# First attention of a four-layer sequence: scores computed a second time with keys on partitions, maxima added by a matmul, exponentials no longer turned

## Chip, cores and metric

The kernel runs on one core of a Trainium2 chip. The metric is the device time of one execution in microseconds; lower is better. The program has four layers; the change touches the first alone, a cross-attention over 16 batches.

## The reference

Layer 0 is a cross-attention with grouped keys. For each of 16 batches, 100 rows of queries (32 heads of 16 channels) look at 361 context rows (8 key and value heads, each shared by four query heads):

```python
q = hidden_state @ Wq + bq                     # (16, 100, 512), 32 heads of 16
k = encoder_hidden_state @ Wk + bk             # (16, 361, 128), 8 heads of 16
v = encoder_hidden_state @ Wv + bv
scores = jnp.einsum('bkgld,bksd->bkgls', q, k) * scale      # scale = 1/4
scores = scores + encoder_attention_mask[:, :, None, :, :]  # a mask per batch, row and key
attn = jax.nn.softmax(scores, axis=-1)
out = jnp.einsum('bkgls,bksd->bkgld', attn, v)
x = out.reshape(b, l, H) @ Wo + bo + hidden_state
return (x - mu) * jax.lax.rsqrt(var + EPS) * gamma + beta
```

Layers 1 and 3 are recurrent blocks, layer 2 is another cross-attention with a feed-forward part. They are not changed. All data is float32.

## The kernel before

Everything is pinned: the helpers `mm` (line 94), `turn` (a transpose on TensorE, line 97) and the wrapped engines `vector`, `scalar`, `gpsimd` (line 89) keep instructions in the order in which the program writes them, engine by engine. So nearly all instructions of the first layer have line 89, 94 or 97 in the profile, and one tells them apart by their tiles.

A batch has 32 heads. A key projection `kz` is written twice, once with the odd and once with the even key heads set to zero (`par01`, a column of ones and zeros per parity), so that a block of 32 partitions holds one key head that counts. Eight steps `x` per batch (two parities `par` by four query groups `q`) make four score tiles each, one for each block `r` of 32 partitions:

- `scores`: four matmuls of 32 rows in four different row groups of the array, which run side by side (a burst), into a ring of four PSUM banks `l0_sc`; rows on partitions, 361 keys along the free axis. Each matmul in float32 is two passes in the profile, so a burst is eight.
- `maximum(r)`: one VectorE instruction adds the mask, writes the negated scores to `pr`, and puts the row's negated maximum into a column of `nm`. In the profile it is CUSTOM_DVE_ANT_0, with a DVE_READ_ACCUMULATOR2_ANT that brings out the maximum.
- `exp(r)`: ScalarE takes the exponential with that maximum as its bias, in place, with the row sum in a column of `sums`.
- `turn_weights`: for the step before, TensorE turns the 100 x 361 weights in three pieces of 121 keys (4 turns a piece, 12 a step) into a ring of two banks `l0_pT`, and ScalarE (two pieces) and VectorE (one) copy them to `pt`, where keys are on partitions.
- `attend`: weights times values, 32 columns of the array per block, summed over both parities in the bank `acc`. The values `vz` have zeros in the other parity's columns.
- `invert` and `divide`: reciprocal of the 32 sums per row, spread to channels by GpSimd, turned by four transposes, multiplied into `y`.
- `output`: four matmuls with `wo`, then the residual, the norm's statistics, scale and shift.

Projections, attend, divide and output are cut into pieces, each with an estimated time and a slot from which it may run; `Filler.run` deals them out to the 24 slots of a batch (three a step) in equal shares, one TensorE piece after another, between the bursts. One bank `m` serves all projections in turn.

Eight PSUM banks: four for scores, two for turned weights, one `acc`, one `m`. The next burst needs all four score banks, and of these the last is freed by the fourth maximum, which stands on VectorE behind the copy of turned weights (cut to the order of calls):

```python
maximum(0)
maximum(1)
due = fill.run(3 * x, due + share)
if last:
    turn_weights(*last[:3], 0)(scalar.copy)
exp(0); exp(1); maximum(2)
due = fill.run(3 * x + 1, due + share)
if last:
    turn_weights(*last[:3], 1)(vector.tensor_copy)
maximum(3)
```

Layer 2's attention (around lines 1550 to 1712) is built in another way: it takes maxima of a first set of scores into a shared scratch tile, turns them, and computes the scores again with keys on partitions.

Of the kernel before, what the change touches and what calls it, by code (L numbers as in the profile page):

```python
# [37 lines left out]
def xattn_sequence(ctx: ExitStack, tc: tile.TileContext, d: dict, out: bass.AP):  # L38
# [313 lines left out]
    def layer0(next_weights, next_small):  # L352
        with ExitStack() as es:
            one = es.enter_context(tc.tile_pool(name="l0_one", bufs=1))
            two = es.enter_context(tc.tile_pool(name="l0_two", bufs=2))
            score = psum_ring(es, "l0_sc", 4)
            turned = psum_ring(es, "l0_pT", 2)
# [10 lines left out]
            par01 = one.tile([128, 2], F32, name="l0_par")  # L368
            bqs = one.tile([128, 4], F32, name="l0_bqs")
            kb = one.tile([128, 2], F32, name="l0_kb")  # L370
            vzs = [one.tile([KW, 3, 2, 128], F32, name=f"vz{i}") for i in range(2)]

            live, qzs, xTs = {}, {}, {}

            def load(b):
                ct = two.tile([128, NC, S2], F32, tag="ct", name=f"ct_{b}")
                nc.sync.dma_start(
                    out=ct,
                    in_=d["ctxT"][:, b * S2 : (b + 1) * S2].rearrange("(c p) s -> p c s", p=128),
                )  # L380
                mask = two.tile([L, S2], F32, tag="mask", bufs=3, name=f"mask_{b}")
                nc.sync.dma_start(out=mask, in_=d["mask0"][b])
                nc.sync.dma_start(out=xb[b], in_=d["x"][b])
                live[b] = {"ct": ct, "mask": mask}
# [81 lines left out]


            def scores(b, x):
                par, q = x // 4, x % 4
                t = live[b]  # L470
                if x == 0:
                    t["nm"] = two.tile([L, 32], F32, tag="nm", name=f"nm0_{b}")
                    t["sums"] = two.tile([L, 32], F32, tag="sums", name=f"sums_{b}")
                    gpsimd.memset(t["sums"], 0.0)
                sl = slice(b % G * L, (b % G + 1) * L)
                ss = [score() for r in range(4)]
                for r in BURST:
                    rs = slice(32 * r, 32 * r + 32)
                    mm(
                        out=ss[r][:L, :S2], lhsT=qzs[b // G][rs, q, sl], rhs=t["kz"][rs, par, :],  # L480
                        start=True, stop=True,
                    )
                pr = two.tile([L, 4, S2], F32, tag="pr", bufs=3, name=f"pr_{b}_{x}")

                def maximum(r):

                    col = 8 * q + 2 * r + par
                    vector.tensor_tensor_reduce(
                        out=pr[:, r, :], in0=ss[r][:L, :S2], in1=t["mask"], scale=-1.0, scalar=FLT_MAX,
                        op0=ALU.add, op1=ALU.min, accum_out=t["nm"][:, col : col + 1],  # L490
                    )

                def exp(r):
                    col = 8 * q + 2 * r + par
                    scalar.activation(
                        pr[:, r, :], pr[:, r, :], AF.Exp, bias=t["nm"][:, col : col + 1], scale=-1.0,
                        accum_out=t["sums"][:, col : col + 1],
                    )

                return pr, maximum, exp  # L500

            def turn_weights(b, x, pr, j):

                par, q = x // 4, x % 4
                t = live[b]
                if q == 0 and j == 0:
                    t["pt", par] = two.tile([KW, 3, 4, T], F32, tag="pt", name=f"pt0_{b}_{par}")
                ps = turned()
                k0 = KEYS[j][0]
                for r in range(4):  # L510
                    turn(ps[:KW, r * L : (r + 1) * L], pr[:, r, k0 : k0 + KW], ident[:L, :L])
                return lambda copy: copy(
                    t["pt", par][:, j, :, q * L : (q + 1) * L],
                    ps[:KW, :T].rearrange("p (r t) -> p r t", t=L),
                )

            def attend(fill, b, par, j, slot):
                n = KEYS[j][1]
                first, last = par == 0 and j == 0, par == 1 and j == 2

                def step():
                    t = live[b]
                    if first:
                        t["acc"] = ps_acc.tile([128, 512], F32, tag="acc", name=f"acc_{b}")
                    for r in range(4):
# [3 lines left out]
                            rhs=t["pt", par][:n, j, r, :], start=first, stop=last,  # L529
                        )  # L530

                def then():
                    t = live[b]
                    t["y"] = two.tile([128, T], F32, tag="y", bufs=1, name=f"y0_{b}")
                    scalar.copy(t["y"], t["acc"][:, :T])

                fill.add(0.8, slot, step, then if last else None, 0)

            def invert(b):

                t = live[b]
                rinv = two.tile([L, 32], F32, tag="rinv", name=f"rinv_{b}")
                vector.reciprocal(rinv, t["sums"])
                t["rx"] = two.tile([L, E], F32, tag="rx", bufs=1, name=f"rx_{b}")
                gpsimd.tensor_copy(
                    t["rx"].rearrange("p (h c) -> p h c", c=16), rinv[:, :, None].to_broadcast([L, 32, 16])
                )

            def divide(fill, b, slot):
                rb = []  # L550

                def step():
                    rb.append(bank(f"rb_{b}"))
                    for q in range(4):
                        turn(
                            rb[0][:, q * L : (q + 1) * L], live[b]["rx"][:, q * 128 : (q + 1) * 128],
                            ident[:L, :L],
                        )

                def then():  # L560
                    y = live[b]["y"]
                    vector.tensor_tensor(y, rb[0][:, :T], y, ALU.mult)

                fill.add(0.5, slot, step, then, 1, object())

            def output(fill, b, slot):
# [6 lines left out]
                def then(t):  # L573
# [3 lines left out]
                    fill.later.append((fill.slot + 2, stats))  # L577

                def stats():
                    st["mv"], st["rstd"] = ln_stats(two, [st["v"]], 1e-6, f"0_{b}", vector, gpsimd)  # L580
                    fill.later.append((fill.slot + 4, scaled))

                def scaled():
# [9 lines left out]
                    fill, 0.88, slot, ps, lambda q: live[b]["y"][:, q * L : (q + 1) * L],  # L593
# [16 lines left out]
            vector.tensor_scalar(kb, par01, bk, None, ALU.mult)  # L610
            for t in vzs:
                gpsimd.memset(t, 0.0)
# [14 lines left out]


            last = None
            for b in range(B + 1):  # L630
                more, more2, prev = b + 1 < B, b + 2 < B, b > 0
                g, bi = b // G, b % G
                if b < B:
                    if more2:
                        load(b + 2)
                    if bi == 0 and g + 1 < NG:
                        load_x(g + 1)
                    if prev:
                        gpsimd.tensor_tensor(xb[b], xb[b], rows[:, 0, :], ALU.add)
                if more:  # L640
                    keys(fill, b + 1)
                if b == 0:
                    values(fill, 0)
                if prev:
                    for j in range(3):
                        attend(fill, b - 1, 1, j, 3 + j)
                if more:
                    values(fill, b + 1, 6)
                if prev:
                    divide(fill, b - 1, 7)  # L650
                    output(fill, b - 1, 9)
                if b < B:
                    for j in range(3):
                        attend(fill, b, 0, j, 15 + j)
                    if bi < 3 and g + 1 < NG:
                        for q in ((0, 1), (2,), (3,))[bi]:
                            queries(fill, g + 1, q, 6)
                share = fill.total() / 24
                due = 0.0
                for x in range(8):  # L660
                    now = (b, x, *scores(b, x)) if b < B else None
                    if now:
                        pr, maximum, exp = now[2:]
                        maximum(0)
                        maximum(1)
                    due = fill.run(3 * x, due + share)
                    if last:
                        turn_weights(*last[:3], 0)(scalar.copy)
                    if now:
                        exp(0)  # L670
                        exp(1)
                        maximum(2)
                    due = fill.run(3 * x + 1, due + share)
                    if last:
                        turn_weights(*last[:3], 1)(vector.tensor_copy)
                    if now:
                        maximum(3)
                    if last:
                        turn_weights(*last[:3], 2)(scalar.copy)
                    if now:  # L680
                        exp(2)
                        exp(3)
                    last = now
                    due = fill.run(3 * x + 2, due + share)
# [1262 lines left out]
```

## Time and profile before

| | |
|---|---|
| three runs | 3127.76, 3128.34 (median), 3133.83 us |
| the profiled execution | 3127.86 us, of which the span of instructions is 3126.1 us |
| granted TensorE clock, mean | 0.961 |
| first scores of the first layer | 39.35 us |
| first instruction of layer 1 that follows the last row of layer 0 | 677.41 us |
| busy in the span: TensorE, VectorE, ScalarE, GpSimd | 91%, 54%, 42%, 37% |
| busy between 39.3 and 677.4 us | 577.0, 361.0, 451.7, 85.4 us |

The page shows one profiled execution. A group line has the line, the engine (PE is TensorE's matmul, PEld its weight load, DVE VectorE, ACT ScalarE, POOL GpSimd), the operation, the tile written and the tiles read, shapes, and the count; behind the bar the busy time of the group, the mean of one in ns, the idle time ahead of it and what ended most of that. Timeline lines start with the start and the length in us. Matmul ends are modelled, so the start of the next group says better how long PE was held.

### The profile page before, as it was taken

The page shows a single profiled execution, that of the slowest core. Times are in us where ns is not written, and L with a number is a line of the kernel's source. Part 1 is how long each engine was busy: PE and PEld are TensorE (multiplying, and loading weights), DVE is VectorE, ACT ScalarE, POOL GpSimd, SP SyncE. Part 2 cuts the span into 40 slices and gives each one's busy share as a digit, 9 for nine tenths or more (in the row PEclk, how much of TensorE's full clock was granted, in tenths as well). Part 3 has the DMA queues.
Part 4 walks back from the last instruction along what each step waited for, and adds up shares of the span by engine and source line. Part 5 has one row for each costly group of instructions (what it writes and reads, how often), then busy time and mean ns, then how long its engine had stood idle before and what let it go on. Part 6 is the DMA issues. An engine that isn't in the chain of part 4 may idle for free. (4 is left out here: it accounts for less than half of the span.)

```text
span 3126.1 us, 44079 instructions
## 1 busy us (share of the span) xinstructions
PE 2858.8 (91%) x16323; PEld 1488.0 (48%) x16323; DVE 1675.5 (54%) x3507; ACT 1308.6 (42%) x2921; POOL 1159.3 (37%) x953
## 2 busy tenths in 40 slices
PE   6999999878889999989999999989999789999998
PEld 3555555534344444444555555455555344444444
DVE  2555556553989988433333333331000369998981
ACT  3777677753435355422222232221111335344553
POOL 0111111133777777412222111220000367787771
PEclk9999999989999999989999999999999889999999
DMA  6010101013224353230000001020002323324321
GB/s 196 24 34 24 34 24 37 3 39 116 80 77 129 96 161 87 71 88 21 21 22 21 21 21 34 28 71 11 11 11 62 101 63 106 109 76 155 105 60 56
DMA packets 139561, 195.93 MB, mean 63 GB/s; under 512 B 23974, under 2 KB 106854, under 8 KB 139346
## 3 DMA queue, kind: packets, MB, share of 16 engines
q1 hardware_dynamic: 116306, 160.34, 17.3%
q10 hardware_dynamic: 23040, 32.78, 2.9%
q8 instruction: 128, 2.10, 0.3%
q14 instruction: 87, 0.71, 0.1%
HBM read 117.16 MB, written 49.15 MB: 53 GB/s over the span
## 5 line engine op out<-in xcount | busy, mean ns | idle before, releaser
L89 POOL TENSOR_TENSOR a<-a,rc 128x800 f32<-128x800 f32 x256 | 487.8, 1908 | 175.8 <-DVE a L89 113.1
L89 DVE TENSOR_TENSOR_SCAN a<-wc,vb 128x400 f32<-128x400 f32 x512 | 477.4, 974 | 28.1 <-PE acc L94 2.2
L89 DVE CUSTOM_DVE_ANT_0 pr<-l_sc,mask 100x361 f32<-100x361 f32 x512 | 252.1, 529 | 148.7 <-PE l_sc L94 148.6
L89 ACT ACTIVATE pr<-pr,nm 100x361 f32<-100x361 f32 x512 | 301.2, 593 | 5.8 <-POOL sums L89 3.7
L89 DVE TENSOR_TENSOR vb<-vb,kc 128x792 f32<-128x792 f32 x256 | 253.8, 991 | 8.8
L97 PEld LDWEIGHTS l_pT<-ident,pr 100*121 100x121 f32 x1536 | 193.3, 186 | 104.3 <-issue 50.9
L1639 DVE CUSTOM_DVE_ANT_0 junk<-l2a_sc,mask 100x361 f32<-100x361 f32 x256 | 136.9, 535 | 182.5 <-PE l2a_sc L94 165.0
L94 PE MATMUL vb<-xc,sel 128*128 128x400 f32 x512 | 207.0, 487 | 18.0 <-DVE a L89 17.8
L97 PE MATMUL l_pT<-ident,pr 100*121 100x100 f32 x1536 | 216.4, 276 | 6.2 <-ACT pt L89 4.3
L1675 POOL TENSOR_TENSOR pa<-pt,pt 121x1600 f32<-121x1600 f32 x16 | 57.1, 3570 | 363.7 <-ACT pt L1670 363.7
L89 ACT COPY pt<-l_pT 121x400 f32<-121x400 f32 x256 | 125.1, 489 | 149.5 <-PE l_pT L97 148.5
L1860 DVE TENSOR_TENSOR x<-pb,x 100x512 f32<-100x512 f32 x16 | 12.6, 790 | 319.9 <-DMA pb<-po 310.1
L89 POOL TENSOR_TENSOR xj<-tm,ext 128x400 f32<-128x400 f32 x160 | 153.6, 981 | 80.1 <-DVE tm L89 59.8
L94 PE MATMUL v<-l_v_w,ct 128*121 128x512 f32 x384 | 177.0, 605 | 0.0
L75 PE MATMUL h<-yTb,l_fc 128*128 128x400 f32 x512 | 172.8, 499 | 0.6 <-ACT yTb L343 0.6
L94 PE MATMUL k<-ct,l_k_w 128*128 128x361 f32 x512 | 170.6, 476 | 0.0
L75 PE MATMUL p<-l_proj,h 128*128 128x512 f32 x384 | 165.5, 592 | 0.0
L89 POOL TENSOR_SCALAR ve<-mv 100x1 f32<-100x1 f32 x16 | 3.6, 224 | 409.8 <-DVE mv L89 409.8
L94 PEld LDWEIGHTS vb<-xc,sel 128*128 128x128 f32 x512 | 97.2, 198 | 109.5 <-issue 36.1
L94 PE MATMUL l_sc<-kz,qz 32*100 32x361 f32 x1024 | 112.6, 509 | 36.1 <-DVE nm L89 33.9
L89 DVE COPY pt<-l_pT 121x400 f32<-121x400 f32 x128 | 73.5, 574 | 132.1 <-PE l_pT L97 64.8
L75 PEld LDWEIGHTS h<-yTb,l_fc 128*128 128x128 f32 x512 | 96.9, 190 | 74.3 <-ACT yTb L343 2.5
(298 smaller groups left out, 5158.0 us busy)
## 6 DMA issues: line engine op xcount, KB each, us to landing
ct<-in_ctxT SPq DMA_DIRECT2D x32, 722.0 KB
dk<-k ACTq DMA_DIRECT2D x32, 200.0 KB
kc<-dk SPq DMA_DIRECT2D x32, 200.0 KB
dv<-v ACTq DMA_DIRECT2D x32, 200.0 KB
dhi<-hi ACTq DMA_DIRECT2D x32, 200.0 KB
dlo<-lo SPq DMA_DIRECT2D x32, 200.0 KB
vc<-dv SPq DMA_DIRECT2D x32, 200.0 KB
dw<-wd ACTq DMA_DIRECT2D x32, 200.0 KB
```

The source lines that it names most:

```text
L75: nc.tensor.matmul(out=ps, lhsT=lhs(c), rhs=rhs(c), start=(c == 0), stop=(c == n - 1))
L89: return lambda *args, **kw: tc.keep_in_program_order(op(*args, **kw))
L94: pin(nc.tensor.matmul(**kw))
L97: pin(nc.tensor.transpose(out, in_, ident))
L1639: nc.vector.tensor_tensor_reduce(out=junk, in0=ss[r][:L, :S2], in1=t["mask"], scale=-1.0, scalar=FLT_MAX, op0=ALU.add, op1=ALU.min, accum_ ...
L1675: nc.gpsimd.tensor_tensor(t["pa"], t["pt"][0], pt, ALU.add)
L1860: nc.vector.tensor_tensor(x, pb[:, i, :], x, ALU.add)
```

## The change

The layer is recut into 32 halves `h` (batch and parity). Each half has seven slots: four of maxima for the next half (`m`) and three of weights for this one (`w`), with the pieces of the filler in between; all of them, and the turns of maxima and of the mask, take their banks from one ring of six.

- `maxima(h, q)`: the score burst as before; the maximum's full output now goes to one shared tile `junk`, the negated maximum to a column of `nms` (two buffers). After the fourth a small copy doubles the columns.
- `turn_maxima(h)`: four turns put the maxima on partitions; ScalarE copies them rounded to fp32r (`high`), VectorE computes what the rounding lost (`parted`).
- `weights(h, j)`: for each piece of 121 keys a second score burst with keys on partitions and 400 columns (four query groups by 100 rows), and onto it a burst with the constant `both` that adds the maxima. The mask, turned once a batch, is added by VectorE for the first `near` of four blocks straight from PSUM, and for the others by GpSimd after a copy by ScalarE. Two exponentials per piece, in place, one and two (or three) slots later.
- The values `vz` have ones instead of zeros in the other parity's columns, so that `attend` yields the sums with the products; each parity has its own accumulation, read by ScalarE into `y` and `s` and added by GpSimd. `divide` exchanges columns with one matmul (`swap`), takes the reciprocal of 128 x 400 on VectorE and multiplies on GpSimd.
- Gone: all turns of weights and their copies, the 32-column sums, `invert` and its spreading and turns.

```diff
-            score = psum_ring(es, "l0_sc", 4)
-            turned = psum_ring(es, "l0_pT", 2)
+            score = psum_ring(es, "l0_sc", 6)
...
-                        out=pr[:, r, :], in0=ss[r][:L, :S2], in1=t["mask"], scale=-1.0, scalar=FLT_MAX,
-                        op0=ALU.add, op1=ALU.min, accum_out=t["nm"][:, col : col + 1],
+                        out=junk, in0=ss[r][:L, :S2], in1=t["mask"], scale=-1.0, scalar=FLT_MAX,
+                        op0=ALU.add, op1=ALU.min, accum_out=nms[par][:, q, col : col + 1],
+                    )
+                if q == 3:
+                    n = nms[par].rearrange("p q (r two s) -> p two s q r", two=2, s=16)[:, 1 - par]
+                    vector.tensor_copy(n[:, 1], n[:, 0])
+
+            def turn_maxima(h):
+                par = h % 2
+                ps = score()
+                for q in range(4):
+                    turn(ps[:, q * L : (q + 1) * L], nms[par][:, q, :], ident[:L, :L])
+                scalar.copy(high, ps[:, :T])
+                return lambda: vector.scalar_tensor_tensor(
+                    parted[par], high, low01[:, par : par + 1], ps[:, :T], ALU.mult, ALU.add
+                )
...
+            def weights(fill, h, j, slot):
...
+                burst(
+                    ss, lambda s: s[:KW, :T].rearrange("p (q t) -> p q t", t=L),
+                    lambda rs: t["kz"][rs, par, k0 : k0 + KW], lambda rs: qzs[b // G][rs, :, sl], stop=False,
+                )
+                burst(
+                    ss, lambda s: s[:KW, :T], lambda rs: both[rs, par, :], lambda rs: parted[par][rs],
+                    start=False,
+                )
+                near = (2, 2, 1)[j]
...
+                for r in range(near):
+                    masked(vector, parts(pt[:, j, r, :]), parts(ss[r][:KW, :T]), 1)
+                for r in range(near, 4):
+                    scalar.copy(pt[:, j, r, :], ss[r][:KW, :T])
+                for r in range(near, 4):
+                    masked(gpsimd, parts(pt[:, j, r, :]), parts(pt[:, j, r, :]), 1)
...
+                fill.later.append((slot + 1, lambda: exp(0, near)))
+                fill.later.append((slot + (2 if j < 2 else 3), lambda: exp(near, 4)))
...
-                    for q in range(4):
-                        turn(
-                            rb[0][:, q * L : (q + 1) * L], live[b]["rx"][:, q * 128 : (q + 1) * 128],
-                            ident[:L, :L],
-                        )
+                    mm(out=sb[0][:, :T], lhsT=swap, rhs=live[b]["s", 0], start=True, stop=True)
...
-                    vector.tensor_tensor(y, rb[0][:, :T], y, ALU.mult)
+                    vector.reciprocal(t["s", 1], sb[0][:, :T])
+                    gpsimd.tensor_tensor(t["y", 0], t["y", 0], t["s", 1], ALU.mult)
...
+            order = (("m", 0), ("m", 1), ("w", 0), ("m", 2), ("w", 1), ("m", 3), ("w", 2))
+            for h in range(-1, 2 * B):
...
+                share = fill.total() / 9
+                due = 0.0
+                for slot, (what, i) in enumerate(order):
+                    if slot == 1 and h >= 0:
+                        part()
+                    if what == "m" and h + 1 < 2 * B:
+                        maxima(h + 1, i)
+                    if what == "w" and h >= 0:
+                        weights(fill, h, i, slot)
+                    due = fill.run(slot, due + share)
+                    if slot == 0 and h >= 0:
+                        part = turn_maxima(h)
+                    if slot == 3 and par and b + 1 < B:
+                        turn_mask(b + 1)
+                fill.carry(7)
```

In halves of the first parity the filler holds the keys of the next batch and the attend of this parity; in those of the second the values of the next batch, this parity's attend, the division and output of the batch, and the queries of the next group of four batches. `share` is the total of the pieces by nine, for seven slots, so that pieces run ahead of need.

## The prediction

> **What bounds the kernel now.** First the page: TensorE (PE) is busy 91% of 3126.1 us, and the first attention, the only stage the change touches, fills slices 1 to 9. The windows view gives that stage alone (columns: length, then busy time of PE, weight loads, VectorE, ScalarE, GpSimd, clock, DMA share, GB/s).
>
> ```profile
> 39.30:677.40 638.10, 576.97 (x4129) 337.73 (x4128) 361.01 (x1258) 451.69 (x1371) 85.40 (x115) 0.98 0.10 31
> 280.00:319.00 39.00, 36.84 (x271) 21.82 (x269) 22.85 (x80) 30.07 (x92) 5.24 (x7) 1.00 0.15 45
> ```
>
> The stage is 638 us: 16 batches of 8 steps, 4.85 us a step (first scores at 39.35, the 128th at 655.50, 127 steps between), then a tail. PE works 36.8 of 39 us of a batch. The timeline shows why the 2.2 us are lost:
>
> ```profile
> 305.34 0.52 DVE L89 CUSTOM_DVE_ANT_0 pr<-l_sc,mask 100x361 f32<-100x361 f32 x1
> 305.79 0.08 DVE L89 DVE_READ_ACCUMULATOR2_ANT nm<- 100x1 f32 x1
> 305.93 0.87 PE L94 MATMUL l_sc<-kz,qz 32*100 32x361 f32 x8
> 306.73 0.88 PE L94 MATMUL acc<-pt,vz 119*32 119x400 f32 x8
> 306.86 0.54 DVE L89 CUSTOM_DVE_ANT_0 pr<-l_sc,mask 100x361 f32<-100x361 f32 x1 [0.99 <-PE l_sc L94]
> 307.32 0.08 DVE L89 DVE_READ_ACCUMULATOR2_ANT nm<- 100x1 f32 x1
> 307.32 0.53 DVE L89 CUSTOM_DVE_ANT_0 pr<-l_sc,mask 100x361 f32<-100x361 f32 x1
> 307.54 1.09 PE L97 MATMUL l_pT<-ident,pr 100*121 100x100 f32 x8
> 308.24 0.49 ACT L89 COPY pt<-l_pT 121x400 f32<-121x400 f32 x1 [1.36 <-PE l_pT L97]
> ```
>
> A score burst needs the bank that the fourth maximum (305.34) frees; PE follows it by 0.06 us (305.87 to 305.93). A burst holds PE 0.80 us, and VectorE reads 0.93 us after its start. Four turns hold PE 0.5 us. The end of the stage counts in full: layer 1 starts when the last row is out, not before.
>
> ```profile
> 676.11 1.26 POOL L89 TENSOR_TENSOR x<-res,l_rows 100x512 f32<-100x512 f32 x1
> 677.41 1.52 ACT L89 ACTIVATE xn_a<-x,fshift,frstd 100x512 f32<-100x512 f32 x2 [10.35 <-POOL x L89]
> ```
>
> Three operations that the first attention gets run already elsewhere, in the second attention: maxima into one shared scratch tile (L1639), the reciprocal of 128x400, and an addition of two tiles on GpSimd.
>
> ```profile
> 1629.91 0.54 DVE L1639 CUSTOM_DVE_ANT_0 junk<-l2a_sc,mask 100x361 f32<-100x361 f32 x1 [1.15 <-PE l2a_sc L94]
> 1630.37 0.08 DVE L1639 DVE_READ_ACCUMULATOR2_ANT nm<- 100x1 f32 x1
> 1630.48 0.53 DVE L1639 CUSTOM_DVE_ANT_0 junk<-l2a_sc,mask 100x361 f32<-100x361 f32 x1
> 1642.87 2.66 DVE L1703 RECIPROCAL y<-sum 128x400 f32<-128x400 f32 x1 [6.21 <-PE sum L94]
> L89 POOL TENSOR_TENSOR xj<-tm,ext 128x400 f32<-128x400 f32 x160 | 153.6, 981 | 80.1 <-DVE tm L89 59.8
> ```
>
> With separate outputs (first fence) maxima follow each other by 0.46 us; with a shared one, where each waits for the one before, by 0.57.
>
> **The work, engine by engine, per batch.** PE loses 96 turns (24 groups of four at 0.5: 12.0 us) and the 4 turns of the inverse (0.5). It gains 6 second score bursts of eight passes over 400 columns (0.81, the row at 306.73: 4.9), 6 bursts of four fp32r passes that add the maxima (half of that, 0.41; the fp32r row vb<-xc,sel has 207.0/512 = 0.40 a pass: 2.4), 11 turns of maxima and mask (1.4) and the swap matmul (0.82). Net 9.5 - 12.5 = -3.0 us: 33.8 of PE. ScalarE: 32 exponentials (593 ns) become 12 longer ones (400 to 1200 columns, about 0.6 to 1.3 by the slope of its copies, 317 ns for 192 and 585 for 512); with copies and the rest about 24 us instead of 30, hidden. VectorE: 32 maxima at 0.57 are 18.3; 10 masked additions from PSUM (575 ns as the y rows) 5.5, two parts of the maxima 1.1, two small copies 0.6, the reciprocal 2.66, layer norm 2.1: 30 instead of 23. GpSimd gets 14 masked additions at 0.98 and three more of that size: 17 more, 22 in all, hidden as long as PE asks for weights late. SP's transfers keep their order and DMA is at 15%: no cost. The setup (a dozen small VectorE operations, memsets) lies under the loads before 39 us; uncovered about 3 us.
>
> So no engine is full (34, 30, 24, 22 of 39). By PE alone the batch would fall from 38.8 to about 36. What decides is how sets of four banks follow each other, because 28 bursts for two halves share six banks.
>
> **The chain of one half (7 slots: m0 m1 w0 m2 w1 m3 w2).** The next burst's last bank is the one that the second reader of the set before frees. So:
> - m to w: 0.93 to the first maximum, 0.57 + 0.54 to the end of the second with its accumulator, 0.06: 2.1 us.
> - w to m: 0.80 + 0.41 + 0.14 until VectorE reads, 0.50 + 0.58 for two masked additions, 0.06: 2.5; after w2 (one addition) 2.0.
> - m0 to m1: between them PE does attend (behind the last far exponential, ready 1.7 after m0; 0.81), two passes of keys (0.72) and the turn of the maxima (0.5): 3.7; then ScalarE's copy (0.5) and VectorE's part of the maxima (0.55) end 1.3 after m1's start and m1's maxima stand behind them on VectorE: +0.3, so 4.0.
>
> The half with keys: 4.0 + 3 x 2.1 + 2 x 2.5 + 2.0 = 17.3 us, of which PE works only 13.7: the rest is handover. The half with values and output has the reciprocal ahead of m0's maxima on VectorE (2.6 us; the values wait for its bank too), and PE's own fillers are long (output pieces 0.90, query pieces 0.81, a third of the values 1.0). In the order m0-m1, m1-w0, w0-m2, m2-w1, w1-m3, m3-w2, w2-end, as the compiled order places the pieces:
> - without queries (6 batches): 4.5 + 2.7 + 3.0 + 3.0 + 2.5 + 2.1 + 2.0 = 19.8
> - one query chain (6): 5.6 + 2.2 + 3.9 + 2.9 + 2.5 + 4.9 + 2.0 = 24.0
> - two (2): 5.6 + 2.2 + 4.8 + 2.1 + 4.5 + 4.0 + 2.0 = 25.2
>
> The first batch, with nothing to attend to or to divide yet, has 16.2 and 21.7. Ahead of it four sets of maxima run alone: 0.93 + 3 x 2.2 + 1.1 = 8.6. The last half has no maxima: its bursts, output pieces and attends end at 13.4, the last far path (copies, three GpSimd additions, an exponential of 1200) at 18.3; then attend 0.8, copies and sums 2.0, swap 0.9, reciprocal 2.7, product 1.0, output 3.7, norm and rows 6.0: 35.4 us. (In before the tail from 660.5 to 677.4 is 16.9, but its last half was a full one.)
>
> Sum: 39.4 + 8.6 + 37.9 + 15 x 17.3 + 6 x 19.8 + 6 x 24.0 + 2 x 25.2 + 35.4 = 694 us against 677.4: +17.
>
> The same replay of a step of before (maxima at 0.93 and 1.39, turns behind the filler, VectorE's copy of the second turn at 3.46, the fourth maximum out at 4.5) gives 4.58 us where 4.85 were measured. The method thus misses between nothing and 6% of 640 us, 0 to 38; since fillers are counted here piece by piece and there by their mean, I take a third, 13: +30. The profiled execution took 3127.86 us (span 3126.1 and 1.8 around it), the median is 3128.34: **3158 us**.
>
> Three prices the trace doesn't show. The strided second scores (32 rows to 121, 400 columns in four pieces): from 0.81 (the acc row) to 1.0 (32 passes of 100 columns in the second attention), taken 0.81, nearest in size; the upper end is 6 x 0.2 x 16 = 19 us. VectorE beside a busier GpSimd: from nothing (its rows from PSUM, 552 to 575 ns, are the same in layer 1) to twice (lo<-v,hi, two SBUF inputs, 1167); the masked additions have one SBUF input, so I take nothing; a tenth would be 32 x 1 = 32 us. A long exponential: 0.83 to 1.0 for 800, mostly covered, below nothing possible if attend starts sooner.
>
> Two rules weighed. The shared scratch tile costs 0.57 against 0.46 a maximum by the rows. The Trainium skill, "VectorE: DVE Perf Modes", "The DRAIN you can't avoid", says a semaphore between Vector operations costs nothing extra; by it the sum would be 4 x 0.11 x 32 = 14 us lower. The two rows of this trace differ, so I keep 0.57. A burst of eight holds PE 0.80 us where one pass alone over 361 columns takes 0.36 (k rows): 3.6-fold packing. "TensorE: Matmul & The Clock Gate", "Measured speedup vs the span model", gives 3.07 for four rows of K=32; by it the new bursts would cost an estimated 30 us more, against the change. The row decides.
>
> **Rivals.**
> - *PE stays the bound.* For it: PE is the fullest engine of the stage and loses 3.0 us a batch; banks rise from four to six and the turned ring goes. Against it: in the half with keys PE has 13.7 us of work in a chain of 17.3. If fillers and handovers overlap better than my chain, the halves sum to 36: 39 + 9 + 15 x 36 + 17 + 35.5 = 640, so -37: **3091 us**, faster. It decides if a pair of halves stays below 38.5 us.
> - *A queue of ScalarE or GpSimd ends last.* Swap waits for GpSimd's sum, that for two ScalarE copies of acc, and those stand behind two kz and two exponentials; I found it ready 0.6 us before PE. A further 1 us a half adds 32: **3190 us**.
> - *The two sides cancel* (a pair near 38.5 us): within 6 us of before.
>
> **Chances.** Forecast 0.57 (its own range 3136 to 3180: 0% and 6%, and the unknown prices), PE-bound 0.26, the queue 0.09, cancelling 0.08. A measurement of this kernel can tell about 0.2%, 6 us, from no change: faster 0.26, same 0.08, slower 0.66. The range for 8 in 10 runs from 3085, which takes in the PE-bound case, to 3190.
>
> **What would show it.** Right: PE busy in the stage (577 us) falls by about 45 us while the stage ends near 707; waits of l_sc for VectorE (82 and 34 us over the stage now) rise several-fold; the maxima are 0.57 apart; VectorE idles about 1 us after each pair of masked additions, for PE; the half with the reciprocal is the longer. Wrong: pairs of halves at 36 to 37 us with PE busy above 92% (first rival), or PE's longest waits on GpSimd or ScalarE (second). If layer 1 starts before 677, the sign was wrong.

## The result, and the profile after

The changed kernel takes **3147.49 us** (median of 5; 3143.77 to 3155.84), the kernel before 3128.60 (median of 5) beside it: a ratio of 1.0063, 95% interval 1.0042 to 1.0083. It is slower by some 19 us. The forecast was 3158, slower. The sign and the range held. What cost the time was only partly what the forecast named: the forecast had the loss in the steady batches, and nearly all of it came at the two ends of the stage.

The profiled execution took 3155.84 us (span 3154.0), the slowest of the five. The windows view of it, for the first attention (39.30 to the start of layer 1), for a half with output and one query chain, and for the half with keys that follows (columns: length, then busy time of PE, weight loads, VectorE, ScalarE, GpSimd, clock, DMA share, GB/s):

```profile
39.30:698.90 659.60, 556.88 (x3888) 234.89 (x3888) 462.66 (x1338) 329.23 (x603) 350.00 (x356) 0.97 0.10 29
307.39:330.14 22.75, 20.32 (x140) 9.39 (x140) 15.86 (x44) 10.65 (x21) 8.84 (x10) 1.00 0.17 42
330.14:347.22 17.08, 14.21 (x106) 5.39 (x106) 13.11 (x42) 10.08 (x19) 12.84 (x12) 1.00 0.14 47
```

Before, PE was busy 577 of 638 us. It now works 20 us less, 557, in a stage that is 21.6 us longer (layer 1 starts at 698.97 instead of 677.41). The timeline shows the chain of one half. First the handover from weights to scores, and the maxima on the shared scratch tile:

```profile
300.30 0.54 DVE L89 CUSTOM_DVE_ANT_0 l_junk<-l_sc,mask 100x361 f32<-100x361 f32 x1
300.76 0.08 DVE L89 DVE_READ_ACCUMULATOR2_ANT nms<- 100x1 f32 x1
300.88 0.53 DVE L89 CUSTOM_DVE_ANT_0 l_junk<-l_sc,mask 100x361 f32<-100x361 f32 x1
...
301.36 0.67 PE L94 MATMUL l_sc<-parted,l_both 32*121 32x400 f32 x4
...
302.10 1.05 DVE L89 TENSOR_TENSOR pt<-l_sc,maskT 121x400 f32<-121x400 f32 x2
...
303.20 0.87 PE L94 MATMUL l_sc<-kz,qz 32*100 32x361 f32 x8 [1.18 <-DVE pt L89]
...
304.14 0.54 DVE L89 CUSTOM_DVE_ANT_0 l_junk<-l_sc,mask 100x361 f32<-100x361 f32 x1 [0.99 <-PE l_sc L94]
...
307.37 2.65 DVE L89 RECIPROCAL s<-s 128x400 f32<-128x400 f32 x1
307.39 0.98 PE L94 MATMUL l_sc<-kz,qz 32*100 32x361 f32 x8 [0.58 <-ACT pt L89]
...
309.93 0.47 DVE L89 CUSTOM_DVE_ANT_0 l_junk<-l_sc,mask 100x361 f32<-100x361 f32 x1
```

The maxima are 0.58 apart. PE stands 1.18 us for the second masked addition, then VectorE stands 0.99 us for PE's new scores: the two take turns. The reciprocal holds back the first maximum of the next half until 2.5 us after its scores began. All this is as forecast. The two ends of the stage are not. The timeline of the run-up and of the tail:

```profile
44.77 0.17 DVE L302 TENSOR_SCALAR gwb<-gwb 128x8 f32<-128x8 f32 x1 [1.60 <-DMA x<-in_x]
...
45.46 1.54 PE L94 MATMUL l_sc<-kz,qz 32*100 32x361 f32 x8 [3.21 <-DVE nms L89]
...
50.38 4.01 PE L94 MATMUL v<-l_wv,ct 128*121 128x128 f32 x24
...
682.14 1.70 PE L94 MATMUL s<-s,l_swap 128*128 128x400 f32 x2 [2.34 <-POOL s L89]
...
683.88 2.66 DVE L89 RECIPROCAL s<-s 128x400 f32<-128x400 f32 x1 [8.80 <-PE s L94]
...
687.76 5.28 PE L94 MATMUL o<-l_wo,y 128*100 128x512 f32 x8 [3.92 <-POOL y L89]
...
698.97 1.52 ACT L89 ACTIVATE xn_a<-x,fshift,frstd 100x512 f32<-100x512 f32 x2 [17.98 <-POOL x L89]
```

A burst that takes 0.87 elsewhere takes 1.54 here, the swap 1.70 instead of 0.94: in places at both ends PE runs at about half speed. And VectorE stands 1.60 us for a DMA at an operation of another part of the program, with maxima behind it.

Cut at the first scores of each half (the last half, which has no scores for maxima, at the turn of its own maxima), the stage (first scores to layer 1) adds up as follows. "Again" is a second profiled execution of the same changed kernel.

| us | run-up | halves 1 and 2 | 14 halves with keys | 14 with output | last with keys | last half and tail | stage |
|---|---|---|---|---|---|---|---|
| predicted | 8.6 | 37.9 | 242.2 | 313.2 | 17.3 | 35.4 | 654.6 |
| after | 15.1 | 40.1 | 240.3 | 301.0 | 24.3 | 39.1 | 659.8 |
| again | 16.2 | 39.0 | 239.3 | 301.0 | 21.5 | 39.7 | 656.8 |
| before | | | the same 14 batches: 539.1 | | | | 638.1 |

The windows view of the 14 steady batches (the second to the fifteenth), before and after:

```profile
85.54:624.62 539.08, 497.27 (x3609) 293.02 (x3608) 315.75 (x1100) 394.11 (x1197) 74.90 (x102) 0.99 0.08 26
94.44:635.66 541.22, 471.89 (x3399) 201.56 (x3398) 403.19 (x1168) 285.64 (x525) 301.40 (x307) 1.00 0.09 26
```

They take 541.2 us, or 38.66 a batch, before 539.1, or 38.5: in all they lose 2 us. The other 20 us of the loss are in the first batch and the last: 659.8 - 541.2 = 118.6 us, against 638.1 - 539.1 = 99.0.

### The profile page after: what moved, and what is told of

Read it like the earlier page. It is cut to its first block, busy times and chain, and to the rows that moved or that the text cites. A ratio compares the mean times of both kernels' runs of the same rounds, so it can differ in the third digit from the quotient of the medians.

```text
span 3154.0 us, 43095 instructions
## 1 busy us (share of the span) xinstructions
PE 2838.8 (90%) x16083; PEld 1383.8 (44%) x16083; DVE 1782.7 (57%) x3598; ACT 1187.0 (38%) x2153; POOL 1424.2 (45%) x1195
## 3 DMA queue, kind: packets, MB, share of 16 engines
q1 hardware_dynamic: 116306, 160.34, 17.3%
## 5 line engine op out<-in xcount | busy, mean ns | idle before, releaser
L89 DVE CUSTOM_DVE_ANT_0 l_junk<-l_sc,mask 100x361 f32<-100x361 f32 x512 | 272.5, 532 | 133.7 <-PE l_sc L94 92.9
L89 POOL TENSOR_TENSOR pt<-pt,maskT 121x400 f32<-121x400 f32 x224 | 227.1, 1038 | 252.2 <-ACT pt L89 252.2
L94 PE MATMUL l_sc<-kz,qz 32*100 32x361 f32 x1024 | 121.2, 515 | 59.9 <-DVE pt L89 34.9
L89 ACT ACTIVATE pt<-pt 121x800 f32<-121x800 f32 (+1 forms) x192 | 161.7, 888 | 1.6 <-POOL pt L89 1.3
L89 ACT COPY pt<-l_sc 121x400 f32<-121x400 f32 x224 | 98.2, 502 | 135.6 <-PE l_sc L94 134.8
L1700 ACT ACTIVATE pt<-l2a_sc,kmask 121x400 f32<-121x400 f32 x192 | 98.4, 595 | 65.6 <-PE l2a_sc L94 65.6
L94 PEld LDWEIGHTS k<-ct,l_k_w 128*128 128x128 f32 x512 | 93.2, 189 | 64.0 <-issue 14.5
```

The source lines that it names most:

```text
L89: return lambda *args, **kw: tc.keep_in_program_order(op(*args, **kw))
L94: pin(nc.tensor.matmul(**kw))
L1700: nc.scalar.activation(pt[:, r, :], st[r][:KW, :T], AF.Exp, bias=t["kmask"][:, j : j + 1], scale=1.0)
```

## The experiments

Theory: the handover of score banks between VectorE and PE sets the half, and PE has slack in it. Rivals: PE is the bound; or a queue of ScalarE or GpSimd ends last. Stage lengths are compared with "again", which ran beside the first three edits.

**The change once more.**

> The changed kernel itself once more, as the base for the three edits beside it: 3140 to 3156 us, the first attention ending at 695 to 700 us and the rest of the program about 2450. If the rest is nearer to the 2449 of the kernel before than the 2455 of the first profile, the 6 us there are the run's own and not the change's.

Measured: 3151.58 us, ratio 1.0079 (1.0062 to 1.0097); layer 1 at 695.25, the rest of the program 2453.05. Over all profiles of this study the rest takes 2441 to 2455 us, whatever the edit in the first attention (2448.7 before). This execution is nearer to the 2455 of the first profile than to before's 2449, so by itself it decides nothing; but the 6 us are within the scatter of all of them, and differences of a few us between two totals can't be placed.

**Four scratch tiles for the maxima.**

```diff
-            junk = one.tile([L, S2], F32, name="l0_junk")
+            junks = [one.tile([L, S2], F32, name=f"l0_junk{i}") for i in range(4)]
...
-                        out=junk, in0=ss[r][:L, :S2], ...
+                        out=junks[r], in0=ss[r][:L, :S2], ...
```

> The scratch tile of the maxima gets four buffers instead of one, so that no maximum waits for the one before it. Theory (the handover of banks sets each half, and the second maximum's end is in every link from scores to weights): maxima 0.46 us apart instead of 0.57, 0.11 us off each of 4 links in 32 halves, 14 us less, about 3133. Rival, the Trainium skill's page (VectorE: DVE Perf Modes, The DRAIN you can't avoid: a semaphore between Vector operations costs nothing extra): 0. Rival, PE or a queue of ScalarE or GpSimd bounds the half: 0.

Measured: **3131.72 us**, ratio 1.0011 (1.0000 to 1.0022). The timeline has its maxima 0.45 to 0.46 apart, each starting at the read of the accumulator before it:

```profile
303.05 0.08 DVE L89 DVE_READ_ACCUMULATOR2_ANT nms<- 100x1 f32 x1
303.05 0.53 DVE L89 CUSTOM_DVE_ANT_0 l_junk<-l_sc,mask 100x361 f32<-100x361 f32 x1
303.50 0.08 DVE L89 DVE_READ_ACCUMULATOR2_ANT nms<- 100x1 f32 x1
303.50 0.53 DVE L89 CUSTOM_DVE_ANT_0 l_junk<-l_sc,mask 100x361 f32<-100x361 f32 x1
```

The stage is 642.8 instead of 656.8 us: 14.0 less, as the theory said. The Trainium skill, "VectorE: DVE Perf Modes", "The DRAIN you can't avoid", found on copies that a semaphore between VectorE's operations costs nothing extra; for these maxima that does not hold. A wait of a maximum for the one just before it, through a shared output, costs about 0.12 us here (0.57 to 0.58 against 0.45 to 0.46 from one to the next), and it was in the path. But the 14 us fell otherwise than reckoned. A half with keys gains 0.55 us instead of 0.44; one with output gains 0.19. That is 10.3 us in the 28 steady halves; the rest fell at the ends, 2.2 us of it in the run-up. Of the 0.55, 0.12 to 0.13 fall in the link m2 to w1 as reckoned and 0.45 in m1 to w0: there the four maxima of m0 stand ahead on VectorE too, and m1's begin 4.7 us after the half's first scores instead of 5.0. So a half with keys is set by the handover, one with output mostly by something else.

**VectorE and ScalarE take turns on the banks.**

```diff
-                for r in range(near):
+                first, rest = ((0, 2), (1, 3)) if j < 2 else ((0,), (1, 2, 3))
+                for r in first:
                     masked(vector, parts(pt[:, j, r, :]), parts(ss[r][:KW, :T]), 1)
-                for r in range(near, 4):
+                for r in rest:
                     scalar.copy(pt[:, j, r, :], ss[r][:KW, :T])
```

> For the first two blocks of keys VectorE takes score banks 0 and 2 and ScalarE with GpSimd banks 1 and 3, instead of 0, 1 and 2, 3; the same operations on every engine. Theory (handover of banks): the second bank is free after one reading (0.5 us) instead of two (1.05), so the link from weights to the next scores falls from 2.3 to about 1.8 in two of three links of 32 halves: 64 x 0.5 = 32 us less at most, 20 to 32 expected, about 3121. Rival, PE is the bound: 0. Rival, ScalarE's queue is last: 0 or slower, since a copy behind an exponential now holds the next scores.

Measured: 3138.52 us, ratio 1.0041 (1.0027 to 1.0056), stage 647.4: 9.4 less, under half of the 20 to 32 that were expected. In a half with keys the first weights link falls from 2.31 to 1.87 as reckoned. The second stays at 2.3 to 2.4, and most halves with output change by 0.25 or nothing. The timeline of that second link shows why, from the scores of the weights at 337.66 to the next scores at 340.06:

```profile
337.66 0.95 PE L94 MATMUL l_sc<-qz,kz 32*121 32x400 f32 x8
...
337.77 0.88 ACT L89 ACTIVATE pt<-pt 121x800 f32<-121x800 f32 x1
...
338.53 0.61 ACT L89 ACTIVATE y<-acc,l_par 128x400 f32<-128x400 f32 x1
...
339.00 0.62 ACT L89 ACTIVATE s<-acc,l_par 128x400 f32<-128x400 f32 x1
...
339.48 0.92 ACT L89 COPY pt<-l_sc 121x400 f32<-121x400 f32 x2
...
340.06 0.87 PE L94 MATMUL l_sc<-kz,qz 32*100 32x361 f32 x8 [1.26 <-ACT pt L89]
```

ScalarE's copies of the banks stand behind an exponential and the two reads of `acc`, and PE waits 1.26 us for them. So the theory holds for one link of the two; in the other ScalarE's queue takes over, the last rival of the expectation.

**Bursts in pairs.**

```diff
-                for r in BURST:
+                for r in order:
...
+                for order in ((0, 1), (3, 2)):
```

> The four groups of a burst are issued in the order 0, 1, 3, 2 instead of 3, 2, 1, 0, and a weights burst as two pairs, each with its maxima behind it. Banks 0 and 1 of a set are long free, so their scores can be made while the set before is still being read. Theory (handover of banks): VectorE's idle microsecond after each pair of masked additions goes, up to 1.05 us in 64 links: 67 us less if two groups run as well packed as four; 30 to 60 less expected, about 3100. Rival, PE is the bound: pairs pack worse than fours, each burst holds PE up to 0.8 us longer, and the kernel becomes slower by 30 to 80 us.

Measured: 3137.2 us, ratio 1.0031 (1.0020 to 1.0042), stage 651.3: 5.5 less. Neither size was right. The windows view, for the same two kinds of half:

```profile
300.88:323.62 22.74, 22.21 (x146) 10.60 (x140) 15.69 (x43) 10.64 (x20) 9.16 (x11) 1.00 0.13 39
323.62:340.10 16.48, 16.34 (x111) 6.83 (x106) 12.80 (x40) 10.07 (x18) 12.68 (x12) 1.00 0.19 53
```

PE is now busy 98 to 99% in both. Pairs cost it 2 us more in a half than bursts of four, which takes back nearly all that the earlier scores gave. With this order PE is the bound; with the order of the change it is not.

**More work for PE in its gap.**

```diff
                         weights(fill, h, i, slot)
+                        if i < 2 and h > 0 and not par:
+                            mm(
+                                out=score(peek=True)[:, :S2], lhsT=wk[:, 0, :],
+                                rhs=live[b]["ct"][:, 0, :], start=True, stop=True,
+                            )
```

> One matmul of 361 columns that nobody reads is added behind the first and the second weights burst of 15 of the 16 halves with keys (two instructions, 0.72 us each time): 21.6 us of PE work in the gap in which PE waits for the masked additions (1.18 us). Theory (handover of banks, PE has slack there): such a half stays at 17.1 us, first attention 0 to 3 us longer. Rival, PE is the bound: 18.5 us a half, 21 us longer.

Measured: 3147.14 us in one execution, stage 656.8, the same as again. The windows view of a half with keys, and of the stretch from 645 us:

```profile
330.56:347.83 17.27, 15.47 (x110) 5.98 (x110) 13.14 (x42) 10.07 (x19) 12.85 (x12) 1.00 0.28 89
645.00:660.00 15.00, 11.78 (x78) 4.03 (x78) 9.33 (x22) 7.98 (x14) 9.70 (x10) 1.00 0.01 1
```

PE works 1.26 us more in the half, and the half is 0.17 longer: PE has slack there, and the rival falls for the halves with keys. The second line holds a surprise. The clock is 1.00, where again has 0.91 in the same stretch:

```profile
645.00:660.00 15.00, 11.31 (x68) 3.64 (x60) 8.95 (x22) 6.46 (x12) 8.01 (x8) 0.91 0.00 0
```

The last half with keys takes 19.45 us instead of 21.53. That the added work did this is not shown: the interleaved readers, with no added work, have 19.26 there.

**Without GpSimd's masked additions.**

```diff
-                for r in range(near, 4):
-                    masked(gpsimd, parts(pt[:, j, r, :]), parts(pt[:, j, r, :]), 1)
```

> GpSimd's masked additions of the far scores are left out (the mask is not added there). Theory: GpSimd is hidden in all halves but the last, so the halves stay at 17.1 and 19.3 to 24.5 us; only the last path of the stage loses its 3.2 us, first attention 2 to 5 us shorter. Rival, GpSimd's queue ends last: every half shorter by 1 us or more, over 30 us in all.

Measured: 3147.02 us in one execution, stage 655.1. The steady halves stay within 0.35 us (two long ones, the seventeenth in count and the last with keys, differ by more, as they do between the two executions of the change). The last half and tail fall from 39.7 to 35.8. GpSimd's queue is not the bound; its part of the second rival falls too, but ScalarE's queue was not tested by this. In one place GpSimd did matter: the norm's scaling on VectorE takes 1022 ns on the mean in after (544 before) and 613 here, and several halves that begin with it go from 17.1 to 16.76. In after a single one takes 0.54 us or 1.23 to 1.36. The first two lines are from after, the other two from the run with four scratch tiles:

```profile
333.14 1.27 POOL L89 TENSOR_TENSOR x<-x,l_rows 100x512 f32<-100x512 f32 x1
...
333.47 1.23 DVE L89 TENSOR_SCALAR res<-res,mv,rstd 100x512 f32<-100x512 f32 x1
...
325.59 0.54 DVE L89 TENSOR_SCALAR res<-res,mv,rstd 100x512 f32<-100x512 f32 x1
325.74 1.52 POOL L89 TENSOR_TENSOR x<-x,l_rows 100x512 f32<-100x512 f32 x1
```

Where GpSimd's addition begins first, the scaling ends 0.29 us behind it; where the scaling begins first, it takes 0.54 and the addition is the longer one.

**PE kept busy at the two ends.**

```diff
+                    if h < 0 and what == "m":
+                        extra(ps_acc.tile([128, 512], F32, tag="acc", name=f"extra_{i}"), 2)
...
+                    if b == B - 1:
+                        extra(score(), 3)
                     mm(out=sb[0][:, :T], lhsT=swap, rhs=live[b]["s", 0], start=True, stop=True)
+                    if b == B - 1:
+                        extra(score(), 5)
```

> Matmuls that nobody reads fill PE's idle time in the run-up (two behind each of the four lone score bursts, 1.45 us each time) and in the tail (three ahead of the last swap, five behind it). Theory (the ends and not the steady halves lose the time, and there PE runs at half speed because it is little busy): the bursts of 1.54 us go to 0.87, the values of 4.0 to 2.0, swap 1.70 to 0.94, output 5.28 to 3.7; run-up 15.1 to about 12, tail 2.4 shorter, 4 to 6 us in all, about 3144. Rival, the clock does not depend on these gaps: the added 11 us of PE work show in part, 0 to 5 us slower.

Measured: 3148.23 us, ratio 1.0049 (1.0032 to 1.0067), whose interval overlaps that of the change; the stage is 655.1, 1.7 less than again and not 4 to 6. The timeline and the windows view (from 40 to 48 us: this run, again, before) show that the clock does depend on the gaps:

```profile
52.09 2.78 PE L94 MATMUL v<-l_wv,ct 128*121 128x128 f32 x24
...
680.68 0.93 PE L94 MATMUL s<-s,l_swap 128*128 128x400 f32 x2
...
685.53 3.68 PE L94 MATMUL o<-l_wo,y 128*100 128x512 f32 x8 [0.89 <-POOL y L89]
```

```profile
40.00:48.00 8.00, 5.69 (x34) 2.45 (x34) 4.43 (x17) 0.59 (x1) 0.00 (x0) 1.00 0.67 210
40.00:48.00 8.00, 3.27 (x19) 1.38 (x19) 5.05 (x21) 0.29 (x1) 0.00 (x0) 0.72 0.73 259
40.00:48.00 8.00, 3.48 (x32) 1.99 (x28) 4.36 (x18) 5.50 (x18) 0.00 (x0) 1.00 0.73 245
```

The clock from 40 to 48 us is 1.00 instead of 0.72, and the last half and tail are 37.1 instead of 39.7, as expected. The run-up falls only from 16.2 to 14.7: VectorE still waits for the DMA at gwb, and one of the added pairs stands in front of the values. And the last half with keys, which the edit does not touch, takes 23.9 instead of 21.5.

**The two steady edits together.**

> Four scratch buffers and the interleaved readers together. Theory: they shorten different links of the same chain, so the stage's gains of 13.7 and 7.6 us add up: it ends near 674, before the 677 of the kernel before, about 3128. Rival, PE (14.2 us of work in a half of 17.1, 20.3 in one of 22.75) takes over: little beyond 681.6, about 3132.

Measured: **3126.04 us** against 3133.07 for the kernel before beside it, ratio 0.9975 (0.9962 to 0.9989): a little faster than before. Layer 1 starts at 674.16. The stage is 633.8, 23.0 less than again, where the two edits alone gave 14.0 and 9.4. In the halves with keys they overlap a little (16.32, from 17.1; 16.51 and 16.77 alone).

**The two ends changed, on top.**

```diff
-        nc.vector.tensor_scalar(gwb, gwb, 0.5, None, ALU.mult)
+        nc.gpsimd.tensor_scalar(gwb, gwb, 0.5, None, ALU.mult)
...
+                alone = h == 2 * B - 1
-                for r in first:
+                for r in range(4) if alone else first:
                     masked(vector, parts(pt[:, j, r, :]), parts(ss[r][:KW, :T]), 1)
```

> On top of the four scratch buffers and the interleaved readers, only the two ends of the stage are changed. Run-up: a scaling of two vectors (gwb) that waits for its DMA goes from VectorE, where maxima stand behind it, to GpSimd, and matmuls that nobody reads fill PE's gaps. Tail: VectorE alone adds the mask in the last half, without ScalarE's copies and GpSimd's additions, and such matmuls stand ahead of the last swap and behind it. Theory (the steady halves are no slower than before's, the two ends lose): halves unchanged at 16.3 and 19.1 to 24.0 us, run-up from 15 to about 11, last half and tail from 39.7 to about 35: first attention 8 us shorter, ending near 666, about 3118. Rival, the ends are set by the loads at the start and by the chain of the last sums, not by these: 0 to 2 us.

Measured: **3113.42 us**, ratio 0.9944 (0.9930 to 0.9957). The halves are unchanged, run-up 11.2, last half and tail 34.4, layer 1 at 665.55. The stage is 7.9 us shorter than with the two steady edits alone, as forecast, through edits that touch no steady half: this part of the loss sat at the ends. The edits at each end were not tried one by one.

**The reciprocal split and moved.**

```diff
-                    vector.reciprocal(t["s", 1], sb[0][:, :T])
-                    gpsimd.tensor_tensor(t["y", 0], t["y", 0], t["s", 1], ALU.mult)
+                    scalar.copy(t["s", 1], sb[0][:, :T])
...
+                    fill.later.append((fill.slot + 1, lambda: part(0, T // 2)))
+                    fill.later.append((fill.slot + 2, lambda: part(T // 2, T)))
```

> On top of the four scratch buffers and the interleaved readers, ScalarE copies the turned sums out of PSUM and VectorE's reciprocal, with its product, is split into two pieces of 200 columns, one behind the first maxima of the half and one behind the second. Theory (the reciprocal of 2.65 us ahead of m0's maxima is in the odd half's chain; m0's first maximum comes 2.5 us after its burst instead of 0.93): each of 14 odd halves 0.9 us shorter, 13 us in all (range 5 to 20), the first attention ending near 661, about 3113. Rival, in these halves PE (17.2 to 20.7 us of work in 19.1 to 22.4) is the bound: under 5 us.

Measured: 3122.02 us, ratio 0.9966 (0.9952 to 0.9979); the stage 5.5 us shorter than without it, of which 3.5 in the 14 halves with output: 0.25 each, not 0.9. The timeline shows why:

```profile
298.27 1.52 PE L94 MATMUL acc<-pt,vz 121*32 121x400 f32 x8
...
298.40 0.54 DVE L89 CUSTOM_DVE_ANT_0 l_junk<-l_sc,mask 100x361 f32<-100x361 f32 x1 [0.97 <-PE l_sc L94]
...
299.72 2.01 PE L94 MATMUL v<-l_wv,ct 128*121 128x128 f32 x16
...
301.56 0.51 PE L97 MATMUL l_sc<-ident,nms 100*128 100x100 f32 x4
302.00 0.87 PE L94 MATMUL l_sc<-kz,qz 32*100 32x361 f32 x8
```

The first maximum now comes 1.0 us after its scores, but PE goes through attend, two thirds of the values and the turn of the maxima before the next scores at 302.00. In this stretch the rival was right: PE's own order sets it.

**All edits, and one edit of the kernel before.**

> All edits together: four scratch buffers, interleaved readers, the split reciprocal, and the two ends. Theory (each shortens its own piece of the chain): halves of 16.3 and 18.8 to 23.8 us as with the split reciprocal, run-up of 11.2 and tail of 34.3 as with the changed ends: first attention 3 to 4 us shorter than with the changed ends alone, ending near 662, about 3110. Rival: 0, with one piece hiding the other.

Measured: **3111.16 us**, ratio 0.9949 (0.9934 to 0.9963), stage 621.6 against 625.9 with the ends alone. The trace has the expected 4 us; the totals can't tell the two kernels apart.

> The kernel before, with only the scaling of gwb moved from VectorE to GpSimd. In its trace VectorE stands 2.63 us at that operation at 44.8 us, with a maximum behind it and the third score burst behind that. Theory: that stall is on the path of a stage that PE bounds afterwards, so the first attention ends 1.5 to 2.6 us sooner, near 675.5, about 3126. Rival: PE's stock of other work takes it up, 0.

Measured: 3128.18 us, ratio 1.0000 (0.9989 to 1.0010). In the one profiled execution, the shortest of the ten, the stage was 4.0 us shorter, but only 0.8 of that in the first batch, where the moved operation stands, and the times show no gain: no support for that part.

## Why the prediction was right, and where it was wrong

The sign and the range held, but not by the sum's reasons. The sum (without its correction) has 555.4 us for the 14 steady batches and 99.2 for the rest of the stage; before has 539.1 and 99.0. So it put the whole loss into the steady batches and none at the ends. Measured were 541.2 and 118.6, the other way round. What held is the mechanism that kept the change from gaining: the halves with keys are set by handovers, and PE's saved work does not show in them. That the total came out slower, and near the forecast, was luck.

- *The chain of a half with keys*: 17.3 forecast, 17.1 measured, link by link 3.56 + 2.63 + 2.31 + 2.10 + 2.31 + 2.48 + 1.71 (the forecast had 4.0, then 2.1, 2.5, 2.1, 2.5, 2.1, 2.0). The single links miss by up to 0.5 and cancel. That handover and not PE sets it is shown: extra PE work costs nearly nothing there, a faster handover shortens it.
- *Halves with output*: 19.8, 24.0 and 25.2 forecast, 19.26, 22.75 and 24.47 measured: 12 us too many over 14 halves. The mis-sized term is m0 to m1, 4.97 instead of 5.6 with one query chain, and m3 to w2, 4.49 instead of 4.9. A steady pair is 38.7 and not 39.7 us. So the third rival, the sides cancel near 38.5, was right for the steady batches.
- *Run-up*: 8.6 forecast, 15.1 measured. Three things were left out: VectorE's stand at gwb, visible in the trace before at 44.81 (2.63 us), PE's half clock, and the values of the first batch, 24 matmuls ahead of the first half (4.01 us here, 2.78 at the full clock in the run with the two ends kept busy). *Last half and tail*: 35.4 against 39.1, *last half with keys* 17.3 against 24.3, both with PE at half speed in places. Before, PE had turns to do there; that the change takes work from PE and so its clock was not in the sum. How much of the loss each of these made was not measured one by one.
- *The correction of 13 us* for the method's miss was wrong. The plain sum put the end of the stage at 694; it came at 698.97 and 695.25. Without it the forecast is 3145, 2.5 us from the median; the errors in the halves and in the ends cancel there.
- *PE's work*: in the steady batches it is busy 471.9 / 14 = 33.7 us, forecast 33.8. But before needs 497.3 / 14 = 35.5 on the mean, and not the 36.8 of the one stretch of 39 us from which the forecast started. So PE lost 1.8 us a batch instead of 3.0; at the ends its busy time rose from 79.7 to 85.0, where half-speed stretches count double. In the stage that is 20 us less, not 45. The waits view has 68.7 + 67.7 + 25.1 + 34.9 = 196 us of waits for VectorE at l_sc, 1.7 times the 116 of before, not several times. Its lines (total, times, longest):

```profile
PEld l_sc L94 <- DVE nms L89: 68.7, 79, 3.8
PEld l_sc L94 <- DVE pt L89: 67.7, 56, 2.1
...
PE l_sc L94 <- DVE pt L89: 34.9, 44, 1.2
...
PE l_sc L94 <- DVE nms L89: 25.1, 44, 3.2
```

- *Prices*: the strided second scores and the matmul of the maxima hold PE 0.46 + 0.60 = 1.06 us, taken as 1.22; VectorE's masked additions from PSUM are not slowed by GpSimd (569 ns, 575 taken). The row `xj`, by which GpSimd's additions were priced, is from the recurrent layers and not from the second attention; the price held (3.01 to 3.03 us for three).
- *PE-bound rival*: it decides only when the pieces of a burst pack worse (pairs), and in the stretch from m0 to m1 of a half with output. *Queue rival*: refuted for GpSimd but for the last half, where its path cost 3.9 us. For ScalarE it is argued from the waits alone: PE and its weight loads wait 30.1 + 15.6 = 46 us for ScalarE at l_sc, against 196 for VectorE.

What stays open: how the 20 us at the ends divide between the clock and the waits, and what sets the scatter of 14 us in the rest of the program.

## What to carry to other kernels

When a change makes a loop's engines hand over to each other and takes work off the busiest one, sum the first and the last round by themselves: the steady rounds here lost 2 us in all, and the ends some 20. Before a shared scratch output is put in a chain, look whether each instruction then waits for the one before it; four small tiles were worth 14 us of the stage. And when a bound engine is relieved, go through its neighbours' in-order queues for foreign instructions that wait for a DMA (what the moved one is worth here was not measured alone: with the added matmuls the run-up fell by 2.5 us, in the kernel before it gave nothing).

## What the hardware showed unexpectedly

- PE's clock fell in gaps of a few microseconds: from 40 to 48 us it was granted 0.72 with 3.27 us of work, and 1.00 with 5.69 (added matmuls). Before had 1.00 there with 3.48, so busy time alone doesn't say it. It fell also in the last half with keys of after, to 0.72 from 635.66 to 659.91, where PE never stood longer than 1.9 us. The Trainium skill, "TensorE: Matmul & The Clock Gate", "What's actually happening", describes a gate with two rates, full and half, opened by activity in windows of about 3.4 us that run freely. The rows 0.87 and 1.54, 0.94 and 1.70 agree with the two rates nearly; no run here shows the windows.
- With the same instructions, the last half with keys took 24.25 us in one execution and 21.53 in another, with the clock granted at 0.72 and 0.84 over it. The run with the two steady edits has 1.00 there and takes 17.49.
- A VectorE scaling of 100x512 in SBUF took 544 ns on the mean before, 1022 with GpSimd busy beside it, and 613 with GpSimd's masked additions left out, while additions that read PSUM stayed at 569. One that begins while a GpSimd addition is under way ends some 0.3 us behind it, so the order in which the two start decides which of them is long.
